# Layer 0's slots turned in 32x32 blocks by VectorE from rows loaded in four pieces, gate and up weights in longer rows, and the two numbers of a row loaded apart in layers 2 and 3

## The chip, the cores and the metric

The kernel runs on one core of one Trainium2 chip. The time is the device time of one execution in microseconds. A core has TensorE (PE, matrix products; its weight loads are listed apart as PEld), VectorE (DVE), ScalarE (ACT), GpSimd (POOL) and SyncE (SP), which here only issues DMAs. Each of them runs its own list of instructions in order, and semaphores hold an instruction back until what it needs is there. Sixteen DMA engines move data between HBM, the on-chip memory of 128 partitions, and back. TensorE contracts over partitions, so it needs activations with channels on partitions ("channel-major"), while rows of a token lie in HBM with a token's channels side by side.

## The reference, cut to what matters

Four layers run on x of 2 x 1024 tokens with 256 channels. Each layer has a conditioning part (a modulation by a vector, attention, or a conditional mixture of experts) and a feed-forward part that is a mixture of experts. Layer 0's feed-forward part is the one that the change reaches most:

```python
topk_ids = jnp.argmax(logits, axis=-1)          # one of E = 32 experts for each of 2048 tokens
xs = x * jax.nn.sigmoid(jnp.max(logits, -1))[:, None]
sorted_x = xs[jnp.argsort(topk_ids)]
g = grouped_mm(sorted_x, routed_gate_w, tokens_per_expert)   # (256 -> 512), called r1
u = grouped_mm(sorted_x, routed_up_w, tokens_per_expert)     # (256 -> 512), called r3
d = grouped_mm(silu(g) * u, routed_down_w, tokens_per_expert)# (512 -> 256), called r2
out = shared_expert(x) + d[argsort(order)]
```

Three more mixtures have the same frame, rows sorted by expert, a small network for each expert, and rows returned to their tokens: layer 2's conditioning (8 experts, two for each token, GELU with 256 hidden channels), layer 2's feed-forward part (8 experts, two for each token, SwiGLU with 1024 hidden channels), and layer 3's conditioning (8 experts, two for each token, GELU with 256 hidden channels).

## The kernel before

**Rows and slots.** Every mixture works on slots of 128 rows. GpSimd scatters token rows into the HBM buffer `xbuf` (`Rows.scatter`, L402). A row has DR = 258 numbers: 256 channels, and two more that say in layers 2 and 3 where the result belongs and whose expert it is. Layer 0 is static: each of its 32 experts owns 96 rows, which makes 24 slots; a token too many goes through a branch (`slots_over`) that is not taken with these inputs. Slots of the other layers are assigned as the routing falls: 35 run in layer 2's conditioning (cph, cpo in the profile), 33 in its feed-forward part, 37 in layer 3's conditioning.

**Loading and turning.** `Slots.fetch` (L1881) loads the 128 x 258 rows of a slot on SyncE's queue (`Rows.load`, L418) into one of four buffers xs. `Slots.rows` (L1889) turns them: two transposes of 128 x 128 on TensorE by `_channel_major` (L500, ps_cm in PSUM), and one VectorE copy out of PSUM (L1895, xsT, three buffers). In layers 2 and 3 two small VectorE operations for each slot then form the row numbers that the result is scattered to: sn (L1899) and sdst (L1902, five buffers), both read from the same buffer xs. `Slots.put` stores a layer 0 result to `ybuf` on ScalarE's queue (L1909), or scatters one of layers 2 and 3 to `tbuf` on GpSimd's.

**Layer 0's order.** `Split.slot` writes TensorE's order by hand: for slot i the gate product fpg (L2081), the up product fpu, then the down product fpo of slot i-1 (L2099), then the turn ps_cm of slot i+2 (L500), then fpt (L2089), four transposes of the product fa of slot i; some preparation of layer 1 is spliced in. VectorE makes fa (L2118), the copy xsT (L1895) and half of faT (L2092); ScalarE makes the SiLU fsg (L2114), the other half of faT and ys (L2103). VectorE also builds layer 1's mask meanwhile (l_ne L901, l_any L903, l_d). The order of VectorE's own instructions is left to a scheduler, which follows what each of them depends on.

**Layer 0's weights.** `ahead` (L553) streams 96 units of 512 KB (gate, up and down of 32 experts) through 22 buffers named ring, XT and HT in the profile, all on SyncE's queue (L559), 21 of them before the first slot. Every unit covers 128 partitions; gate and up lie there as two rows of 2 KB to a partition, down as four of 1 KB.

**Layers 2 and 3.** `Series.slot` is the loop: rows of slot n+2 are fetched, slot n+1 is turned, the weights of slot n are loaded (`_expert_load`, L1865, only for an expert that no set holds), then come the products of slot n. `_gelu_products` (cph L1976, cpo L1983, ys L1985) serves the two conditioning mixtures, `_ffn_products` (L2000 to L2009) and `_mixed_products` layer 2's feed-forward part.

Of the kernel before, what the change touches and what calls it, by code (L numbers as in the profile page):

```python
# [9 lines left out]
F32 = mybir.dt.float32  # L10
I32 = mybir.dt.int32
U32 = mybir.dt.uint32
# [29 lines left out]
class Ring:  # L42


    def __init__(self, t, n):
        self.t, self.n, self.i, self.held = t, n, 0, set()
# [339 lines left out]
class Rows:  # L386
# [30 lines left out]
    def load(self, dst, src):  # L417
        i = self.k.nc.sync.dma_start(dst, src)  # L418
        _after(self.k, i, self.new)
        self.read.append(i.ins.name)  # L420
        return i
# [70 lines left out]
    return ps.rearrange("p c d -> p (c d)")  # L492


def _channel_major(k, psum, rows, ref=None, made=None):


    ps = psum.tile([P, 2, P], F32, name="ps_cm", tag="t", bufs=2)
    for c in range(2):
        i = k.nc.tensor.transpose(ps[:, c, :], rows[:, c * P:(c + 1) * P], k.ident)  # L500
        if ref is not None:
            _behind(k, i, ref)
        if made is not None:
            made.append(i)
    return ps
# [19 lines left out]
def _layer0(k):  # L525
# [14 lines left out]
    def weights(src):  # L540
        ws = [k.ring.take().rearrange("p (c f) -> p c f", f=f) for f in (F, F, D)]
        for w, n in zip(ws, ("L0_r1", "L0_r3", "L0_r2")):
            sent.append(nc.sync.dma_start(w, A[n][src].rearrange("o (c p) f -> p (o c) f", p=P)))
        return ws


# [6 lines left out]
    def ahead(free, ref=None):  # L553

        while todo and 3 * todo[0][0] + todo[0][1] - len(units) < free:
            e, j = todo.pop(0)
            n, f = kinds[j]
            w = ws[e][j] = units[(3 * e + j) % len(units)].rearrange("p (c f) -> p c f", f=f)
            sent.append(nc.sync.dma_start(w, A[n][e].rearrange("(c p) f -> p c f", p=P)))  # L559
            if ref is not None:  # L560
                _behind(k, sent[-1], ref)

    with ExitStack() as ctx:
# [93 lines left out]
        _layer1_loads0(k, k.pre)  # L657
        ahead(-2)
        slots = Slots(k, pool, psum, ref=sent[-1])
        split = Split(k, pool, psum, slots, F, NS)  # L660
        muls = []
        mask = _mask_rows(k, k.pre, pool, psum, muls)
        pre = chain(_layer1_pre(k, k.pre, psum, split.stage), _router_biases(k, psum, split.stage))
        for i in range(NS):
            if i < 18 and i % 2 == 1:
                next(mask)
            lo, cols = i * T, []
            while lo < (i + 1) * T:

                e = lo // C  # L670
                n = 64 if i % 3 == 1 else 32
                cols.append((slice(lo - i * T, lo - i * T + n), ws[e]))
                lo += n
            muls.append(split.slot(i, cols))
            next(pre, None)

            ahead(3 * (i * T // C), slots.load)
        with k.tc.issue_after(split.up.ins):
            k.tc.mark_branch_hint_location('rare', 'LikelyTaken', [mybir.EngineType.PE])
        assert next(pre, pre) is pre and not todo  # L680
# [1192 lines left out]
class Slots:  # L1873

    def __init__(self, k, pool, psum, of=None, base=0, ref=None):
        self.k, self.pool, self.psum, self.of, self.base, self.ref = k, pool, psum, of, base, ref
        self.xs, self.dst = {}, {}

    def fetch(self, i):  # L1881

        if i not in self.xs:
            self.xs[i] = self.pool.tile([P, DR], F32, name="xs", bufs=4)
            self.load = self.k.x.load(self.xs[i], self.k.xbuf[i * P:(i + 1) * P, :])
            if self.ref is not None:
                _behind(self.k, self.load, self.ref)

    def rows(self, i, made=None):  # L1889

        k, nc, pool = self.k, self.k.nc, self.pool
        self.fetch(i)
        xs = self.xs.pop(i)
        xT = pool.tile([P, 2, P], F32, name="xsT", bufs=3)
        turned = nc.vector.tensor_copy(xT, _channel_major(k, self.psum, xs, made=made))  # L1895
        if self.of is not None:

            n = pool.tile([P, 1], F32, name="sn", bufs=3)
            j = nc.vector.tensor_tensor(n, xs[:, D + 1:D + 2], self.of[:, i:i + 1], ALU.not_equal)  # L1899
            _behind(k, j, turned)  # L1900
            self.dst[i] = pool.tile([P, 1], U32, name="sdst", bufs=5)
            j = nc.vector.scalar_tensor_tensor(self.dst[i], xs[:, D:D + 1], -float(self.base), n,  # L1902
                                               ALU.add, ALU.add)
            _behind(k, j, turned)
        return xT

    def put(self, i, y):
        if self.of is None:
            self.k.nc.scalar.dma_start(self.k.ybuf[i * P:(i + 1) * P, :], y)  # L1909
        else:  # L1910

            self.k.t.scatter(y, self.dst.pop(i), bounds_check=2 * N - 1, oob_is_err=False)


class Series:
# [1 line left out]

    def __init__(self, k, slots, ids):  # L1920
        self.k, self.slots, self.ids = k, slots, list(ids)
        self.xT, self.last, self.old, self.soon = {}, None, None, False
        self.fetch(0)
        self.fetch(1)
        self.turn(0)

    def stage(self, insts):

        for i in insts:
            if self.last is not None:  # L1930
                _behind(self.k, i, self.last)
        self.last = insts[-1]

    def fetch(self, n):
        if n < len(self.ids):
# [8 lines left out]
    def slot(self, i, products, weights, soon=False):  # L1944

        n = self.ids.index(i)
        self.fetch(n + 2)
        self.turn(n + 1)
        if self.soon:
            self.close()  # L1950
        self.soon = soon
        p = products(self.xT.pop(i), *weights())
        self.stage(next(p))
        self.close()
        part = next(p)
        while part is not None:
            self.stage(part)
            self.part = part
            part = next(p)
        self.old = i, p  # L1960
# [101 lines left out]
class Split:  # L2062
# [9 lines left out]
    def stage(self, insts):  # L2072

        for i in insts:
            if self.last is not None:
                _behind(self.k, i, self.last)
        self.last = insts[-1]

    def product(self, name, xT, cols, j):
        ps = self.psum.tile([P, self.F], F32, name=name, tag="mm")  # L2080
# [58 lines left out]
def _cond_moe(k, name, wr, bias, W1, W3, W2, nf, hold, R1, R2, gate_mult, final, lead, most, next=None):  # L2139
# [70 lines left out]
        shared(tb, hook, lead_.mid, between=lead_.between)  # L2210
    gate, eid, of, used = lead_.finish()
    k.t.begin()
    by = Slots(k, pool, psum, of, base)

    def slots(lo, hi):
        series = Series(k, by, range(lo, hi))
        for i in range(lo, hi):
            series.slot(i, _gelu_products(k, pool, psum), lambda: _slot_weights(k, eid, i, sets, E))
        series.close()
# [41 lines left out]
def _layer2_ffn(k):  # L2261
# [55 lines left out]
        shared(tb, lead.hook, lead.mid, lead.between)  # L2317
    gate, eid, of, used, mid = lead.finish()
    k.t.begin()
    by = Slots(k, pool, psum, of, base)  # L2320

    def weights(i):
        to = sets[i % 2] if i < MOST - 1 else sets[(i + 1) % 2]
# [3 lines left out]
        return [_expert_load(k, mid, 3 * m + q, sets[j], E) for q, j in enumerate(to) if j is not None]  # L2327

    def slots(ids):
        series = Series(k, by, ids)  # L2330
        for n, i in enumerate(ids):
            if i == NS:
                series.slot(i, _mixed_products(k, pool, psum), lambda: mixed(0, 0, 1, 2), True)
            elif i > NS:
                series.slot(i, _mixed_products(k, pool, psum), lambda: [ahead[0], *mixed(1, None, 0, 1)],
                            True)
            else:
                series.slot(i, _ffn_products(k, pool, psum, 2), lambda: weights(i))
            if i == 8:
                ahead = mixed(1, 2)  # L2340
            if i == MOST - 1:
                with k.tc.issue_after(series.part[len(series.part) // 2].ins):
                    k.tc.mark_branch_hint_location('l2f', 'LikelyTaken', [mybir.EngineType.PE])
        series.close()
# [15 lines left out]
class Last:  # L2360
# [535 lines left out]
```

## Time and profile before

| what | value |
|---|---|
| median of 10 executions | 1414.31 us (1411.46 to 1418.48) |
| the profiled execution | 1415.73 us, its span 1414.0 us |
| mean granted clock of TensorE | 0.988 |
| TensorE busy | 1364.5 us, 96% |
| VectorE, ScalarE, GpSimd busy | 33%, 21%, 19% |
| layer 0's slots, TensorE in 177 to 212 us | 35.00 of 35 us, DMA share 1.05 |
| layer 2's conditioning slots, 441.08 to 512.0 us | TensorE 68.36 of 70.92 us |
| layer 3's conditioning slots, 1176.89 to 1252.81 us | TensorE 72.61 of 75.92 us |

The profiled execution is one execution; its span runs from the first to the last instruction, and the rest of its time lies outside. In the views below a line of the timeline has a start and a length in microseconds, the engine, the line of the kernel, the operation, what it writes and reads, and in brackets how long the engine was idle before it and what ended that. A line of the busy times has the stretch, its length, then each engine's busy time with its number of instructions, the granted clock, the mean busy share of the 16 DMA engines (which can pass 1, as overlapping packets count twice), and the rate. A line of the waits has what waited for what, the total, the number of waits and the longest.

### The profile page before, as it was taken

The page shows a single profiled execution, that of the slowest core. Times are in us where ns is not written, and L with a number is a line of the kernel's source. Part 1 is how long each engine was busy: PE and PEld are TensorE (multiplying, and loading weights), DVE is VectorE, ACT ScalarE, POOL GpSimd, SP SyncE. Part 2 cuts the span into 40 slices and gives each one's busy share as a digit, 9 for nine tenths or more (in the row PEclk, how much of TensorE's full clock was granted, in tenths as well). Part 3 has the DMA queues.
Part 4 walks back from the last instruction along what each step waited for, and adds up shares of the span by engine and source line. Part 5 has one row for each costly group of instructions (what it writes and reads, how often), then busy time and mean ns, then how long its engine had stood idle before and what let it go on. Part 6 is the DMA issues. An engine that isn't in the chain of part 4 may idle for free. (4 is left out here: it accounts for less than half of the span.)

```text
span 1414.0 us, 23096 instructions
## 1 busy us (share of the span) xinstructions
PE 1364.5 (96%) x8431; PEld 955.8 (68%) x8431; DVE 461.5 (33%) x1519; ACT 302.1 (21%) x636; POOL 273.1 (19%) x308
## 2 busy tenths in 40 slices
PE   9999999999999999999999999999999979998897
PEld 4544444655657876555599999999956548875685
DVE  3523322325313443511211111111115503458432
ACT  3212221234112112111111111111112212127121
POOL 0410001300432430142000001000100262430441
PEclk9999999999999999999999999999999989999899
DMA  9879992933313861081375365366338346748570
GB/s 309 309 236 348 357 367 76 305 84 135 113 52 88 254 201 54 29 314 61 101 286 206 111 209 205 118 235 226 119 117 299 115 137 213 239 148 281 196 236 16
DMA packets 185424, 265.26 MB, mean 188 GB/s; under 512 B 16759, under 2 KB 134655, under 8 KB 185296
## 3 DMA queue, kind: packets, MB, share of 16 engines
q1 hardware_dynamic: 163984, 221.65, 47.6%
q0 software_dynamic: 13744, 36.63, 7.3%
q10 hardware_dynamic: 7568, 5.34, 1.2%
q8 instruction: 71, 1.16, 0.3%
q14 instruction: 57, 0.47, 0.1%
HBM read 283.67 MB, written 46.82 MB: 234 GB/s over the span
## 5 line engine op out<-in xcount | busy, mean ns | idle before, releaser
L402 POOL DMA_INDIRECT tbuf<-ys,sdst x105 | 103.3, 984 | 466.8 <-ACT ys L2012 300.9
L1675 PE MATMUL spo<-ring,sa 128*128 128x256 f32 x704 | 167.7, 384 | 9.6 <-DVE sa L1703 9.5
L1675 PEld LDWEIGHTS spo<-ring,sa 128*128 128x128 f32 x704 | 134.2, 193 | 56.3 <-issue 28.3
L1703 DVE TENSOR_TENSOR sa<-ssg,spu 128x512 f32<-128x512 f32 x88 | 60.3, 686 | 248.6 <-PE spu L1690 203.3
L2005 DVE TENSOR_TENSOR fa<-fsg,fpu 128x512 f32<-128x512 f32 x62 | 42.6, 688 | 278.3 <-PE fpu L2000 278.3
L2000 PE MATMUL fpg<-xsT,ring 128*128 128x128 f32 x992 | 121.1, 275 | 1.0 <-DMA ring<-in_L_w 1.0
L2000 PE MATMUL fpu<-xsT,ring 128*128 128x128 f32 x992 | 121.0, 275 | 0.6 <-DMA ring<-in_L_w 0.6
L2000 PEld LDWEIGHTS fpg<-xsT,ring 128*128 128x128 f32 x992 | 117.9, 192 | 3.5 <-issue 2.0
L2000 PEld LDWEIGHTS fpu<-xsT,ring 128*128 128x128 f32 x992 | 115.7, 192 | 0.7 <-issue 0.7
L1699 ACT ACTIVATE ssg<-spg 128x512 f32<-128x512 f32 x88 | 52.5, 597 | 282.0 <-PE spg L1690 220.0
L2009 PE MATMUL fpo<-ring,fa 128*128 128x256 f32 x496 | 112.4, 380 | 0.0
L2009 PEld LDWEIGHTS fpo<-ring,fa 128*128 128x128 f32 x496 | 91.9, 190 | 12.1 <-issue 0.8
L1690 PE MATMUL spg<-HT,ring 128*128 128x512 f32 x192 | 92.8, 598 | 4.1 <-issue 2.2
L1690 PE MATMUL spu<-HT,ring 128*128 128x512 f32 x192 | 91.2, 598 | 0.0
L1976 PE MATMUL cph<-xsT,ring 128*128 128x128 f32 x576 | 77.5, 277 | 5.9 <-DVE sn L1899 2.6
L1690 PE MATMUL spg<-XT,ring 128*128 128x512 f32 x160 | 75.6, 594 | 1.3 <-DVE ys L1985 1.2
L1976 PEld LDWEIGHTS cph<-xsT,ring 128*128 128x128 f32 x576 | 70.1, 192 | 9.3 <-DVE sn L1899 4.1
L1690 PE MATMUL spu<-XT,ring 128*128 128x512 f32 x160 | 75.4, 592 | 0.0
L1983 PE MATMUL cpo<-ring,ch 128*128 128x256 f32 x288 | 73.8, 380 | 0.0
L2004 ACT ACTIVATE fsg<-fpg 128x512 f32<-128x512 f32 x62 | 37.0, 597 | 143.8 <-PE fpg L2000 142.5
L1690 PEld LDWEIGHTS spu<-HT,ring 128*128 128x128 f32 x192 | 36.7, 193 | 45.1 <-issue 44.9
L1895 DVE COPY xsT<-ps_cm 128x256 f32<-128x256 f32 x129 | 53.8, 418 | 30.5 <-PE ps_cm L500 30.5
(677 smaller groups left out, 1761.8 us busy)
## 6 DMA issues: line engine op xcount, KB each, us to landing
ring<-in_L_w SPq DMA_DIRECT2D x105, 1024.0 KB
ring<-in_L_r SPq DMA_DIRECT2D x72, 512.0 KB
ring<-in_L_r SPq DMA_DIRECT2D x144, 256.0 KB
xs<-xbuf SPq DMA_DIRECT2D x129, 129.0 KB
ring<-in_L_W SPq DMA_DIRECT2D x32, 512.0 KB
yt<-tbuf SPq DMA_DIRECT2D x48, 256.0 KB
XT<-in_L_r SPq DMA_DIRECT2D x16, 512.0 KB
HT<-in_L_r SPq DMA_DIRECT2D x8, 512.0 KB
```

The lines of the kernel that those rows point to most:

```text
L402: i = k.nc.gpsimd.indirect_dma_start(out=self.ap, out_offset=bass.IndirectOffsetOnAxis(ap=idx, axis=0), in_=rows, in_offset=None, **end)
L1675: mm = nc.tensor.matmul(po[g // 2][:, g % 2, :], a[:, g * P:(g + 1) * P], W2[:, f, :], start=f == 0 and g % 2 == 0, stop=f == nf - 1, skip ...
L1690: mm = nc.tensor.matmul(ps, W[:, c, f * P:(f + 1) * P], X[:, c, cols], start=c == 0, stop=c == 1)
L1699: k.silu = nc.scalar.activation(sg, pg, AF.Silu)
L1703: mul = nc.vector.tensor_mul(a, sg, pu)
L1895: turned = nc.vector.tensor_copy(xT, _channel_major(k, self.psum, xs, made=made))
L1976: made = [nc.tensor.matmul(ph[:, f, :], R1[:, c, f * P:(f + 1) * P], xT[:, c, :], start=c == 0, stop=c == 1) for f in range(2) for c in ra ...
L1983: made = [nc.tensor.matmul(po, h[:, f, :], R2[:, f, :], start=f == 0, stop=f == 1) for f in range(2)]
L2000: made = [nc.tensor.matmul(ps[:, j, :], W[:, c, (f0 + j) * P:(f0 + j + 1) * P], xT[:, c, :], start=c == 0, stop=c == 1) for ps, W in ((pg, ...
L2004: nc.scalar.activation(sg, pg, AF.Silu)
L2005: nc.vector.tensor_mul(a[:, f0:f0 + 4, :], sg, pu)
L2009: made = [nc.tensor.matmul(po, a[:, f, :], W2[:, f, :], start=f == 0, stop=f == 4 * nh - 1) for f in range(4 * nh)]
```

## The change

The change has four edits.

1. *Layer 0's turn.* Slots 2 to 23 are loaded by four DMAs instead of one. DMA q brings channels 64q to 64q+63 of all 128 rows to the 32 partitions 32q to 32q+31, four pieces of 256 B to a partition (`xq`). One VectorE transpose, which turns every 32x32 block in place, then writes xsT directly. The TensorE transposes and the PSUM copy of these slots are gone. Partition p now holds channels 2p and 2p+1, and so slots 0 and 1, which stay on TensorE, read every second channel (`pairs`).
2. *Weights.* Gate and up of layer 0 are laid down to match: one row of 4 KB to a partition. Down is as before.
3. *Numbers.* In layers 2 and 3 (`blocks=False`, so TensorE still turns) a row load brings 256 channels. The two numbers of all rows of a stage come in one DMA (`numbers`, called once after the turn of the stage's second slot), 128 partitions by 39 or 41 slots by 8 B, in a buffer of the xs pool; two VectorE operations form all row numbers of the stage at once, and each scatter uses a column of them.
4. *Fetching.* `Series.slot` asks for the rows of slot n+3 behind the weights of slot n.

```diff
 def _channel_major(..., pairs=False):
-        i = k.nc.tensor.transpose(ps[:, c, :], rows[:, c * P:(c + 1) * P], k.ident)
+        i = k.nc.tensor.transpose(ps[:, c, :], rows[:, c::2] if pairs else rows[:, c * P:(c + 1) * P], k.ident)
...
-            sent.append(nc.sync.dma_start(w, A[n][e].rearrange("(c p) f -> p c f", p=P)))
+            form = "(c p) f -> p c f" if n == "L0_r2" else "(p c) f -> p c f"
+            sent.append(nc.sync.dma_start(w, A[n][e].rearrange(form, p=P)))
...
         slots = Slots(k, pool, psum, ref=sent[-1])
+        slots.plan(range(NS), (0, 1), 1)
...
     def fetch(self, i):
-        if i not in self.xs:
-            self.xs[i] = self.pool.tile([P, DR], F32, name="xs", bufs=4)
-            self.load = self.k.x.load(self.xs[i], self.k.xbuf[i * P:(i + 1) * P, :])
...
+        if group is None:
+            self.xs[i] = self.pool.tile([P, D], F32, name="xs", bufs=4)
+            self.load(self.xs[i], k.xbuf[i * P:(i + 1) * P, 0:D])
+            return
+        lo, n = group
+        if self.of is None:
+            t = self.pool.tile([P, n, 4, 64], F32, name="xq", tag="xs", bufs=4)
...
+        for q in range(4):
+            self.load(t[32 * q:32 * q + 32, 0:n].rearrange("p g b k -> p (g b) k"),
+                      k.xbuf[lo * P:(lo + n) * P, 64 * q:64 * q + 64].rearrange("(b s) k -> s b k", s=32))
...
     def rows(self, i, made):
-        turned = nc.vector.tensor_copy(xT, _channel_major(k, self.psum, xs, made=made))
-        if self.of is not None:
-            n = pool.tile([P, 1], F32, name="sn", bufs=3)
-            j = nc.vector.tensor_tensor(n, xs[:, D + 1:D + 2], self.of[:, i:i + 1], ALU.not_equal)
-            _behind(k, j, turned)
-            self.dst[i] = pool.tile([P, 1], U32, name="sdst", bufs=5)
-            j = nc.vector.scalar_tensor_tensor(self.dst[i], xs[:, D:D + 1], -float(self.base), n,
-                                               ALU.add, ALU.add)
+        if self.group[i] is None:
+            self.turned = nc.vector.tensor_copy(xT, _channel_major(k, self.psum, xs, made=made, pairs=self.blocks))
+        else:
+            self.turned = nc.vector.transpose(xT.rearrange("p c (b s) -> p c b s", b=4),
+                                              xs.rearrange("p b (r c) -> p c b r", c=2))
...
+    def numbers(self):
+        k, nc, n = self.k, self.k.nc, self.of.shape[1]
+        m = self.pool.tile([P, n, 2], F32, name="xm", tag="xs", bufs=4)
+        k.x.load(m, k.xbuf[0:n * P, D:].rearrange("(i p) d -> p i d", p=P))
+        i = nc.vector.tensor_tensor(m[:, :, 1], m[:, :, 1], self.of, ALU.not_equal)
+        _behind(k, i, self.turned)
+        self.dst = k.rp.tile([P, n], U32, name="sdst", tag="sdst")
+        nc.vector.scalar_tensor_tensor(self.dst, m[:, :, 0], -float(self.base), m[:, :, 1], ALU.add, ALU.add)
...
     def slot(self, i, products, weights, soon=False):
         n = self.ids.index(i)
         self.fetch(n + 2)
         self.turn(n + 1)
+        if self.slots.of is not None and self.slots.dst is None:
+            self.slots.numbers()
...
         p = products(self.xT.pop(i), *weights())
+        self.fetch(n + 3)
...
-    by = Slots(k, pool, psum, of, base)
+    by = Slots(k, pool, psum, of, base, blocks=False)
```

More of the change, by code (lines that the diff above doesn't have):

```diff
@@ L492, in _token_major, with _channel_major @@
     return ps.rearrange("p c d -> p (c d)")
-def _channel_major(k, psum, rows, ref=None, made=None):
+def _channel_major(k, psum, rows, ref=None, made=None, pairs=False):
     ps = psum.tile([P, 2, P], F32, name="ps_cm", tag="t", bufs=2)
     for c in range(2):
-        i = k.nc.tensor.transpose(ps[:, c, :], rows[:, c * P:(c + 1) * P], k.ident)
+        i = k.nc.tensor.transpose(ps[:, c, :], rows[:, c::2] if pairs else rows[:, c * P:(c + 1) * P], k.ident)
         if ref is not None:
@@ L542, in weights @@
         for w, n in zip(ws, ("L0_r1", "L0_r3", "L0_r2")):
-            sent.append(nc.sync.dma_start(w, A[n][src].rearrange("o (c p) f -> p (o c) f", p=P)))
+            form = "o (c p) f -> p (o c) f" if n == "L0_r2" else "o (p c) f -> p (o c) f"
+            sent.append(nc.sync.dma_start(w, A[n][src].rearrange(form, p=P)))
         return ws
@@ L675, in _layer0 @@
             next(pre, None)
-            ahead(3 * (i * T // C), slots.load)
+            ahead(3 * (i * T // C), slots.loaded)
         with k.tc.issue_after(split.up.ins):
@@ L1873, with __init__, plan, load @@
 class Slots:
-    def __init__(self, k, pool, psum, of=None, base=0, ref=None):
+    def __init__(self, k, pool, psum, of=None, base=0, ref=None, blocks=True):
         self.k, self.pool, self.psum, self.of, self.base, self.ref = k, pool, psum, of, base, ref
-        self.xs, self.dst = {}, {}
-    def fetch(self, i):
-        if i not in self.xs:
-            self.xs[i] = self.pool.tile([P, DR], F32, name="xs", bufs=4)
-            self.load = self.k.x.load(self.xs[i], self.k.xbuf[i * P:(i + 1) * P, :])
-            if self.ref is not None:
-                _behind(self.k, self.load, self.ref)
-    def rows(self, i, made=None):
+        self.xs, self.group, self.dst, self.blocks = {}, {}, None, blocks
+    def plan(self, ids, rows, most):
+        ids = list(ids)
+        while ids:
+            n = 1
+            if ids[0] in rows or not self.blocks:
+                self.group[ids[0]] = None
+            else:
+                while n < most and ids[n:n + 1] == [ids[0] + n]:
+                    n += 1
+                for j in range(n):
+                    self.group[ids[j]] = ids[0], n
+            ids = ids[n:]
+    def load(self, t, src):
+        self.loaded = self.k.x.load(t, src)
+        if self.ref is not None:
+            _behind(self.k, self.loaded, self.ref)
+    def fetch(self, i):
+        if i in self.xs:
+            return
+        k, group = self.k, self.group[i]
+        if group is None:
+            self.xs[i] = self.pool.tile([P, D], F32, name="xs", bufs=4)
+            self.load(self.xs[i], k.xbuf[i * P:(i + 1) * P, 0:D])
+            return
+        lo, n = group
+        if self.of is None:
+            t = self.pool.tile([P, n, 4, 64], F32, name="xq", tag="xs", bufs=4)
+        else:
+            t = self.pool.tile([P, 2, 4, 64], F32, name="xq", tag="yt", bufs=5)
+        for q in range(4):
+            self.load(t[32 * q:32 * q + 32, 0:n].rearrange("p g b k -> p (g b) k"),
+                      k.xbuf[lo * P:(lo + n) * P, 64 * q:64 * q + 64].rearrange("(b s) k -> s b k", s=32))
+        for j in range(n):
+            self.xs[lo + j] = t[:, j]
+    def rows(self, i, made):
         k, nc, pool = self.k, self.k.nc, self.pool
@@ L1894, in rows @@
         xT = pool.tile([P, 2, P], F32, name="xsT", bufs=3)
-        turned = nc.vector.tensor_copy(xT, _channel_major(k, self.psum, xs, made=made))
-        if self.of is not None:
-            n = pool.tile([P, 1], F32, name="sn", bufs=3)
-            j = nc.vector.tensor_tensor(n, xs[:, D + 1:D + 2], self.of[:, i:i + 1], ALU.not_equal)
-            _behind(k, j, turned)
-            self.dst[i] = pool.tile([P, 1], U32, name="sdst", bufs=5)
-            j = nc.vector.scalar_tensor_tensor(self.dst[i], xs[:, D:D + 1], -float(self.base), n,
-                                               ALU.add, ALU.add)
-            _behind(k, j, turned)
-        return xT
+        if self.group[i] is None:
+            self.turned = nc.vector.tensor_copy(xT, _channel_major(k, self.psum, xs, made=made, pairs=self.blocks))
+        else:
+            self.turned = nc.vector.transpose(xT.rearrange("p c (b s) -> p c b s", b=4),
+                                              xs.rearrange("p b (r c) -> p c b r", c=2))
+        return xT
+    def numbers(self):
[6 more added lines that the diff above has]
+        nc.vector.scalar_tensor_tensor(self.dst, m[:, :, 0], -float(self.base), m[:, :, 1], ALU.add, ALU.add)
     def put(self, i, y):
@@ L1910, in put, with __init__ @@
         else:
-            self.k.t.scatter(y, self.dst.pop(i), bounds_check=2 * N - 1, oob_is_err=False)
+            self.k.t.scatter(y, self.dst[:, i:i + 1], bounds_check=2 * N - 1, oob_is_err=False)
 class Series:
-    def __init__(self, k, slots, ids):
+    def __init__(self, k, slots, ids, rows=0):
         self.k, self.slots, self.ids = k, slots, list(ids)
         self.xT, self.last, self.old, self.soon = {}, None, None, False
+        slots.plan(ids, self.ids[:rows], 1 if slots.of is None else 2)
         self.fetch(0)
@@ L1931, in stage @@
                 _behind(self.k, i, self.last)
-        self.last = insts[-1]
+        self.last = (insts or [self.last])[-1]
     def fetch(self, n):
@@ L2076, in stage @@
                 _behind(self.k, i, self.last)
-        self.last = insts[-1]
+        self.last = (insts or [self.last])[-1]
     def product(self, name, xT, cols, j):
@@ L2212, in _cond_moe @@
     k.t.begin()
-    by = Slots(k, pool, psum, of, base)
+    by = Slots(k, pool, psum, of, base, blocks=False)
     def slots(lo, hi):
-        series = Series(k, by, range(lo, hi))
+        series = Series(k, by, range(lo, hi), 0 if lo else 2)
         for i in range(lo, hi):
@@ L2319, in _layer2_ffn @@
     k.t.begin()
-    by = Slots(k, pool, psum, of, base)
+    by = Slots(k, pool, psum, of, base, blocks=False)
     def weights(i):
@@ L2329, in slots @@
     def slots(ids):
-        series = Series(k, by, ids)
+        series = Series(k, by, ids, 1 if ids[0] == NS else 0)
         for n, i in enumerate(ids):
```

## The prediction

> **What bounds the kernel now.** I read the page first, then the busy time of each engine by stretch, then the timeline of the last slots of layer 0 and of the first slots of layer 3's mixture, and last the waits of SyncE's queue. From the page:
>
> ```profile
> PE 1364.5 (96%) x8431; PEld 955.8 (68%) x8431; DVE 461.5 (33%) x1519; ACT 302.1 (21%) x636; POOL 273.1 (19%) x308
> PE   9999999999999999999999999999999979998897
> DMA  9879992933313861081375365366338346748570
> q10 hardware_dynamic: 7568, 5.34, 1.2%
> ```
>
> TensorE is the bound nearly everywhere. Layer 0's slots (slices 2 to 6) have both TensorE and the DMA engines full, so a microsecond off TensorE there counts only while weights keep up. Busy time by stretch (columns: stretch, length, PE, PEld, DVE, ACT, POOL, clock, DMA share, GB/s):
>
> ```profile
> 7.00:10.00 3.00, 2.15 (x11) 1.57 (x12) 2.65 (x10) 0.21 (x1) 0.00 (x0) 1.00 1.06 403
> 177.00:212.00 35.00, 35.00 (x342) 14.93 (x336) 10.12 (x24) 7.30 (x16) 0.00 (x0) 1.00 1.05 368
> 250.00:266.00 16.00, 16.00 (x57) 9.78 (x56) 6.72 (x14) 3.08 (x7) 8.37 (x9) 1.00 1.14 298
> 441.08:512.00 70.92, 68.36 (x475) 61.87 (x474) 35.42 (x137) 14.91 (x36) 31.49 (x32) 1.00 0.67 208
> 1176.89:1252.81 75.92, 72.61 (x504) 65.58 (x503) 37.18 (x145) 15.67 (x38) 33.47 (x34) 1.00 0.71 226
> ```
>
> Layer 0 has no PE gap (177 to 212); the slots of layers 2 and 3 (last two lines) have gaps of 2.6 and 3.3 us. The turns that move, in the timeline (start, length, engine, line):
>
> ```profile
> 200.75 1.94 PE L2081 MATMUL fpg<-ring,xsT 128*64 128x512 f32 x8
> 206.20 0.44 PE L500 MATMUL ps_cm<-ident,xs 128*128 128x128 f32 x2
> 206.67 0.42 DVE L1895 COPY xsT<-ps_cm 128x256 f32<-128x256 f32 x1 [1.48 <-PE ps_cm L500]
> 207.00 1.92 PE L2081 MATMUL fpg<-ring,xsT 128*32 128x512 f32 x16
> ...
> 219.36 0.64 PE L2081 MATMUL fpg<-XT,xsT 128*64 128x512 f32 x1
> 224.81 0.66 PE L2089 MATMUL fpt<-ident,fa 128*128 128x128 f32 x4
> 225.39 0.62 PE L2081 MATMUL fpg<-HT,xsT 128*32 128x512 f32 x1
> 225.50 0.42 DVE L2092 COPY faT<-fpt 128x256 f32<-128x256 f32 x1 [1.70 <-PE fpt L2089]
> ```
>
> The copy at 206.67 is for a slot that starts over 6 us later: today the turned rows are a slot ahead. Also needed are the spacing of two mask operations on VectorE, the start of layer 3's slots, and SyncE's waits (total, times, longest):
>
> ```profile
> 161.69 0.42 DVE L901 TENSOR_TENSOR l_ne<-l_mm,l_m 128x256 int32<-128x256 int32 x1
> 162.15 0.42 DVE L903 TENSOR_TENSOR l_any<-l_any,l_ne 128x256 int32<-128x256 int32 x1
> ```
> ```profile
> 1173.64 5.42 SPq L418 DMA_DIRECT2D xs<-xbuf  x6
> 1179.26 0.42 DVE L1895 COPY xsT<-ps_cm 128x256 f32<-128x256 f32 x1 [0.80 <-PE ps_cm L500]
> 1181.04 1.06 PE L1976 MATMUL cph<-xsT,ring 128*128 128x128 f32 x8
> ```
> ```profile
> SPq L418 <- DVE sdst L1902: 70.3, 43, 23.9
> ```
>
> **Part 1, TensorE's turns in layer 0.** 22 of 24 slots lose their ps_cm pair. Slots 19 and 22 have the same column split: 19, with a pair, runs 200.75 to 207.00 = 6.25 us; 22, the first without one (no slot 24 exists), 219.36 to 225.39 = 6.03. Saved 0.22 a slot, 22 x 0.22 = **-4.8 us**. Bounds: slot 21 (6.11) against 22 gives 0.08, -1.8; the pair's own 0.44 gives -9.7. I take 0.22, the like-for-like pair.
>
> The Trainium skill, "VectorE: DVE Perf Modes", section "The three transpose paths", gives 390 ns for a 128x128 bf16 transpose on TensorE and 311 ns on VectorE, the latter in 32x32 blocks only. By it TensorE would save 22 x 2 x 0.39 = 17 us (an estimate), but it prices a transpose alone; the trace shows the pair overlapped with its neighbours.
>
> **Part 2, the turn on VectorE.** The new instruction reads what the DMA laid down, so the schedule no longer ties it to a place on TensorE. In the built order it slips: up to slot 10 it stands one or more products ahead of need, but from slot 11 slot n's turn comes after the product fa(n-1), just before slot n's fpg, which waits for it. Behind fa(n-1) alone it is covered by fpo(n-2) (1.93 us). For n = 14, 20, 23 it stands behind faT(n-1) too: faT starts 0.69 after fpt (224.81, 225.50), the turn 0.34 later (spacing of 206.67's kind of copy), ends 0.42 on, and PE starts 0.06 after: fpt + 1.51, where fpg comes now at + 0.58. That is 0.93 each, 2.8. For n = 11 and 17 two mask operations (0.46 and 0.34 more) stand between: 1.7 each, 3.4. n = 19 stands behind layer 1's l_d chain, which waits for PE: about 0.7. Sum **+6.9 us**. Its duration is not in the trace; nearest are the 128x256 f32 copy and int32 operation, both 0.42, which I take. Bounds: 0.33 (the shortest 128x256 spacing), and 0.84 (two of them), which adds 6 x 0.42 = 2.5. If the scheduler's places do not bite, 0. Bounds 0 to +9.4. The 22 PSUM copies go, and cost nothing: DVE is 10.12 of 35 busy.
>
> **Part 3, DMA in layer 0.** A slot's rows become 512 pieces of 256 B in four DMAs on 32 partitions. At 403 GB/s a 2 KB row takes 2048 x 16 / 403 = 81 ns per engine; at 298 GB/s, in the stretch of 512 B rows, 27.5. The line through both is 10 ns a descriptor plus 0.035 ns/B. So (512 - 128) x 10 / 16 = +0.24 us a slot. ACT's queue gives a dearer end: 1.2% x 16 x 1414 / 7568 = 36 ns each, which would make it 0.86. Against it, gate and up in 4 KB rows save 256 descriptors an expert, 341 a slot: -0.21. Net about 0 to +0.65 us of 6.25 a slot, up to 14 in all. The last weight is issued at 207.43 and needed at 225.39, about 14 us after landing, and SyncE waits for PE before weights (35.8 us in 17 waits): **0**. SyncE issues three more DMAs a slot, about 0.4 each, beside four weights of 0.45 to 1.1: full, but not over 6 us. At the start 14 row issues stand before the HT weights instead of 5, at 0.58 (2.91 / 5): those weights are 5 us later, of 14 us slack; slot 2's pieces land about 77.70 + 6 x 0.58 + 2.15 = 83.3 (2.15 from issue to PE today), and VectorE needs them before fa0 at 84.58. If all this cover went, +1 to +6.
>
> The Trainium skill, "DMA: Bandwidth & Descriptors", section "Rules for kernel authors", says that transfers to separate parts of the partitions serialize and advises one over 128; its "Specifications" ask for at least 512 B for line rate. Both speak against this edit. No row here has 256 B pieces at full load, so the descriptor line above decides the sum, and the page's advice would only raise the risk of starving.
>
> **Part 4, the numbers in layers 2 and 3.** Each stage now loads the two numbers of all slots with one DMA of 4992 or 5248 pieces of 8 B, 313 or more an engine, and VectorE's one pair on them stands before the turn of slot 2. So cph(2) and all of VectorE wait for its landing. Per piece: 10 ns (line), 15.5 (ACT's queue less its 1 KB rows: (271 - 233) us / 2448), 36 (its mean): 3.3, 4.9, 11.3 us, and 2.15 to land. In layer 3's slots it is issued about 1175.0 and needed by about 1180.25 (VectorE's turn, copy and hand-over take 0.8 before 1181.04): late by 0.2, 1.8 or 8.2. I take **+1.8**. Layer 2's cond slots have 10.7 us of cover (0; 2.7 at 36 ns), its ffn 24 (0).
>
> Gone are 105 pairs of small VectorE operations and their waits. A slot's sdst waited for an old scatter to finish, and so held its xs buffer and SyncE's queue (70.3 us over 43 waits). What TensorE lost by this is unclear: an undisturbed slot of the cph stages takes 1.98 us from cph to cph (1179.06 to 1181.04), and against that the two stages lose 3.6 and 4.7 = 8.3 us. The gaps lie where every slot brings new weights and the DMA share is 1.0 or more (1.00 to 1.07 between 1184 and 1202 and 1216 and 1228), so they are lack of bandwidth; a queue freed sooner only starts such a burst sooner, by what sdst held it (SyncE's longest such wait there is 1.8 us). Bounds 0 to -8.3; I take **-1.5**, less than one such hold per stage. The extra fetch(n+3) keeps the order of rows and weights on SyncE as it was: 0. The 105 turns there stay on PE.
>
> **Sum**: -4.8 + 6.9 + 0 + 1.8 - 1.5 = +2.4. The profiled execution took 1415.73 (span 1414.0, 1.73 outside it); it would take 1418.1. It lies 1.42 above the median 1414.31, so I forecast 1416.7.
>
> **Rivals.** (a) Faster: the freed queue. If sdst's release recovers over 6.7 of the 8.3 us, the sum falls below -2.8; all of it gives -4.4, 1409.9. For it: 70.3 us of waits; against: PE's own gaps on sn are 2.6 us on the page. (b) The 8 B pieces cost 36 ns: 8.2 + 2.7 in place of 1.8, 1425.8. For it: ACT's mean; against: that mean holds 1 KB rows. (c) Weights starve in layer 0: +1 to +6, 3.5 in the middle, 1420.2. For it: DMA share 1.05; against: 14 us of slack. (d) The late turns don't stall, because hardware reaches them sooner than the order suggests or they are short: 1414.3 - 4.8 + 1.8 - 1.5 = 1409.8; with the stalls under 1.7 us it ends below -2.8. For it: VectorE is idle for two thirds of layer 0; against: the order of the built program. (e) The change does not do what it says, TensorE's time per slot not falling since weights set the pace: 4.8 more, 1421.5; for it, the full DMA row of 177 to 212, against it, SyncE's waits for PE. It is counted with (c).
>
> **How the numbers follow.** About 0.2% either way (2.8 us) can be told from no change. Forecast 0.45 (0.22 slower, 0.23 same, as its sum lies beside the bound); (a) 0.13 (0.11 faster, 0.02 same); (b) 0.16, slower; (c) with (e) 0.12 (0.10 slower, 0.02 same); (d) 0.14 (0.11 faster, 0.03 same). Together faster 0.22, same 0.30, slower 0.48. The range 1409.0 to 1424.0 leaves out most of (b) and the ends of (a) and (d) in which bounds add up. The forecast's own range is 1413.5 to 1420.5.
>
> **What would show it.** After: PE gaps before fpg of slots 11, 14, 17, 19, 20, 23, released by VectorE's transpose; slots with an early turn near 6.03; no fpg released by DMA (else c); layer 3's cph(2) released by sdst or xm's DMA; SyncE's wait for sdst near 0. The forecast is wrong if the transpose takes over 0.84 us, if pieces cost other than 10 to 15 ns, or if the gaps of the later slots close.

## The result

The changed kernel takes 1439.14 us (median of 8 runs, 1434.78 to 1442.04); the kernel before, beside it, 1414.61 (28 runs). The ratio is 1.0171, 95% interval 1.0157 to 1.0184: slower by some 24 us. The forecast was 1416.7, with a range up to 1424.0. The profiled execution took 1439.78 us, its span 1438.1.

The page of the changed kernel, in the lines that answer to those shown before:

```profile
PE 1368.0 (95%) x8387; PEld 953.7 (66%) x8387; DVE 434.0 (30%) x1315; ACT 302.1 (21%) x636; POOL 273.3 (19%) x308
PE   9999787999999999999999999999999978998897
DMA  9858888793222663082284556256448346848570
```

TensorE now idles in slices 5 to 7, which are the second half of layer 0's slots; before, every one of them was 9. The DMA row fell from 9 to 8 in slices 4 to 6, and in slice 7 it is 8 where it was 2: the same weights arrive over a longer time. So the DMA engines did not become the bound: they are less busy than before while TensorE waits. The busy times by stretch say the same (columns as before). First two stretches of the kernel before, of which the prediction shows the third (1.05, 368 GB/s):

```profile
106.00:141.00 35.00, 35.00 (x362) 16.25 (x362) 11.98 (x34) 9.94 (x20) 0.00 (x0) 1.00 1.02 348
141.00:177.00 36.00, 36.00 (x352) 15.39 (x345) 11.51 (x24) 7.74 (x18) 0.00 (x0) 1.00 1.04 357
```

Then the changed kernel:

```profile
106.00:141.00 35.00, 35.00 (x362) 15.56 (x362) 10.53 (x31) 10.08 (x19) 0.00 (x0) 1.00 0.83 279
141.00:177.00 36.00, 28.39 (x264) 11.47 (x252) 8.66 (x18) 6.11 (x14) 0.00 (x0) 0.98 0.78 255
177.00:212.00 35.00, 30.29 (x235) 11.71 (x239) 7.57 (x16) 5.37 (x12) 0.00 (x0) 0.87 0.88 296
212.00:252.00 40.00, 32.36 (x290) 13.34 (x282) 8.98 (x22) 6.71 (x15) 0.00 (x0) 1.00 0.84 276
```

From the starts of products in the two timelines, the 24.1 us between the spans come from these places:

| stretch | before, us | after, us | difference |
|---|---|---|---|
| span's start to slot 0's fpg | 80.78 | 81.22 | +0.4 |
| fpg of slot 0 to fpg of slot 23 | 144.61 | 171.40 | +26.8 |
| from there to layer 2's first cph | 216.68 | 212.68 | -4.0 |
| layer 2's cond slots, first to last cph | 69.93 | 68.16 | -1.8 |
| between the two cph stages | 665.88 | 666.34 | +0.5 |
| layer 3's cond slots | 74.93 | 76.98 | +2.1 |
| the rest | 161.19 | 161.32 | +0.1 |

Not all of the 26.8 us in the slots is waiting. From slot 0's to slot 23's fpg TensorE is idle for 21.5 us (0.5 before). Beside that the profile shows half the clock granted in two stretches, where before it was 1.00 through all these slots:

```profile
175.87:182.70 6.83, 5.61 (x28) 1.57 (x32) 0.45 (x1) 0.60 (x1) 0.00 (x0) 0.50 1.03 311
203.18:206.59 3.41, 3.09 (x16) 0.92 (x20) 0.17 (x1) 0.00 (x0) 0.00 (x0) 0.50 1.02 393
```

Slot 14, in which TensorE never idles, has 5.6 us of this and takes 8.79 us, against 6.04 in the fourth experiment below. Half of the 10.2 us, some 5 us (an estimate), is thus lost to the clock and not to a wait. In the profiles in which rows and weights come in time (the kernel before and the first, third, fifth, sixth, seventh and ninth experiments) no such stretch lies in the slots; which wait brings it on was not tried.

The waits of SyncE's queue, then those of TensorE, between 80 and 256 us of the changed kernel (total, times, longest):

```profile
SPq L418 <- DMA ybuf<-ys: 44.2, 8, 8.1
SPq L561 <- DMA ybuf<-ys: 17.0, 6, 7.4
...
PE fpg L2124 <- DVE xsT L1932: 15.3, 5, 4.6
PE fpg L2124 <- DMA ring<-in_L_r: 2.4, 2, 2.2
PE fpg L2124 <- issue: 1.6, 1, 1.6
```

SyncE, which loads rows (L418) and weights (L561), spends 61 us waiting for ybuf, the stores of results that ScalarE's queue makes, although no row and no weight needs a result. One such wait in full, from the timeline of SyncE's queue and of the engines that follow from it:

```profile
160.69 5.45 SPq L561 DMA_DIRECT2D ring<-in_L_r  x6
166.25 7.92 SPq L418 DMA_DIRECT2D xq<-xbuf  x4
174.21 1.47 SPq L561 DMA_DIRECT2D ring<-in_L_r  x3
...
176.50 0.45 DVE L1932 STREAM_TRANSPOSE xsT<-xq 128x256 f32<-128x256 f32 x1 [2.48 <-DMA xq<-xbuf]
177.09 1.93 PE L2124 MATMUL fpg<-ring,xsT 128*32 128x512 f32 x8 [3.54 <-DVE xsT L1932]
```

SyncE's longest wait between 160 and 176 us:

```profile
SPq L418 <- DMA ybuf<-ys: 5.6, 1, 5.6
```

Four row DMAs of 0.4 us each take 7.92 us, because the third stands 5.6 us for a store. In the built program every DMA that SyncE or ScalarE issues has one of eight semaphores that tell of its landing, taken in rotation by both engines together; the trace shows the same eight on both queues. A DMA waits until the one that last used its semaphore has landed, which is the one some eight places back. The third row DMA here, issued at 173.38, takes the semaphore of the store that ScalarE issued at 166.51. Its pieces land late, VectorE turns late, and TensorE stands 3.54 us. The weights behind it on the queue are held too.

With one row DMA a slot some six DMAs belong to a slot (one of rows, four of weights, one store), so that SyncE could be more than a slot ahead of the store it waits for; with four there are nine, and eight places are less than a slot. Before, the same wait was in the profile (stretch 80 to 232, SyncE), but SyncE had the lead to bear it:

```profile
SPq L559 <- DMA ybuf<-ys: 14.6, 8, 4.4
```

This is the theory "shared semaphores". Its rivals are "late turns" (the prediction's own part 2), "pieces" (256 B pieces fill the DMA engines) and "weights" (the longer weight rows).

### The profile page after: what moved, and what is told of

It reads as the page before. It is cut to its first block, busy times and chain, and to the rows that moved or that the text cites. A ratio compares the mean times of both kernels' runs of the same rounds, so it can differ in the third digit from the quotient of the medians.

```text
span 1438.1 us, 22941 instructions
## 1 busy us (share of the span) xinstructions
PE 1368.0 (95%) x8387; PEld 953.7 (66%) x8387; DVE 434.0 (30%) x1315; ACT 302.1 (21%) x636; POOL 273.3 (19%) x308
## 5 line engine op out<-in xcount | busy, mean ns | idle before, releaser
L2028 DVE COPY ys<-cpo 128x256 f32<-128x256 f32 x72 | 30.6, 425 | 93.5 <-PE cpo L2026 78.2
```

The costliest lines, as they stand in the source:

```text
L2028: nc.vector.tensor_copy(y, po)
```

## The experiments

**Stores from GpSimd.** In the built program GpSimd's DMAs take no part in this rotation (they have eight other semaphores), so this takes the stores out of it.

```diff
     def put(self, i, y):
         if self.of is None:
-            self.k.nc.scalar.dma_start(self.k.ybuf[i * P:(i + 1) * P, :], y)
+            self.k.nc.gpsimd.dma_start(self.k.ybuf[i * P:(i + 1) * P, :], y)
```

> The changed kernel, with layer 0's result stores (ybuf) issued from GpSimd instead of ScalarE. Theory 'shared semaphores': in the built program every DMA of SyncE and ScalarE waits for the DMA that stands eight places earlier in one common rotation; with four row DMAs a slot, SyncE reaches a result store that has not been written yet, stops there (44.2 + 17.0 us of its waits name ybuf) and issues weights late. Taking the stores out of the rotation should give back most of the 24.5 us: 1417 to 1427. Rival 'late turns': PE waits because VectorE's turn stands behind other work; no change, 1437 to 1441. Rival 'pieces': the 256 B pieces fill the DMA engines; no change, 1437 to 1441.

Measured: 1418.69 us beside 1417.29, ratio 1.0012 (0.9994 to 1.0030). Of 24 us, about 23 are gone. "Pieces" and "weights" fall as main causes: both are still in. What is left shows the late turns by themselves. TensorE's waits for them between 80 and 256 us, which lie before slots 11, 14, 17, 20 and 23, and then the end of slot 18:

```profile
PE fpg L2124 <- DVE xsT L1932: 6.4, 5, 1.8
```
```profile
200.17 0.69 DVE L2161 TENSOR_TENSOR fa<-fsg,fpu 128x512 f32<-128x512 f32 x1 [2.46 <-PE fpu L2124]
...
201.22 0.15 DVE L909 TENSOR_SCALAR l_d<-l_d 128x1 f32<-128x1 f32 x1
...
201.43 0.38 PE L911 MATMUL l_pd<-l_d,ones 128*128 128x1 f32 x2
...
201.85 0.16 DVE L913 COPY l_differf<-l_pd 128x1 f32<-128x1 f32 x1 [0.47 <-PE l_pd L911]
...
202.29 0.14 DVE L687 CAST l_rare<-l_raref 1x1 int32<-1x1 f32 x1
202.47 0.45 DVE L1932 STREAM_TRANSPOSE xsT<-xq 128x256 f32<-128x256 f32 x1
202.74 0.66 PE L2132 MATMUL fpt<-ident,fa 128*128 128x128 f32 x4
203.33 1.51 PE L2124 MATMUL fpg<-ring,xsT 128*64 128x512 f32 x6
```

In slot 18 the turn stands behind fa and the l_d chain, as the prediction read it from the built order. But slot 19's fpg does not wait for this turn: it comes 0.59 us behind fpt, as in a slot without a stall. The slot's 1.0 us is lost earlier, where TensorE's own step of the chain (l_pd, L911) stands in the middle of fpo and needs l_d: fpt starts 6.35 us after the slot's fpg, and 5.30 in the fourth experiment, in which no l_d stands in this slot.

**The number of DMAs alone, without pieces and without VectorE's turn.** The kernel before, its rows in four DMAs of 32 whole rows.

```diff
-            self.load = self.k.x.load(self.xs[i], self.k.xbuf[i * P:(i + 1) * P, :])
...
+            for q in range(4 if self.of is None else 1):
+                r = slice(32 * q, 32 * q + 32) if self.of is None else slice(0, P)
+                self.load = self.k.x.load(self.xs[i][r, :], self.k.xbuf[i * P + r.start:i * P + r.stop, :])
```

> The kernel before, with each slot's rows in layer 0 loaded by four DMAs of 32 whole rows instead of one of 128 (same 128 rows of 1032 B, turns on TensorE, everything else as before). Shared semaphores: the number of DMAs alone costs most of the loss, 1426 to 1438. Late turns and pieces: nothing of theirs is in it, 1413 to 1416.

Measured: 1440.27 us beside 1417.29 (4 runs), ratio 1.0173 (1.0134 to 1.0213), just above the expected range. The number of DMAs makes as large a loss by itself, with old pieces, old weight rows and old turns. (3.5 of TensorE's 18.2 us below lie before slot 0's first product; the clock is below 1 here too.) The waits between 80 and 256 us of TensorE and SyncE, and two stretches:

```profile
PE ps_cm L500 <- DMA xs<-xbuf: 18.2, 7, 4.4
...
SPq L418 <- DMA ybuf<-ys: 31.7, 6, 7.0
```
```profile
177.00:212.00 35.00, 29.39 (x252) 12.52 (x256) 10.92 (x27) 5.75 (x13) 0.00 (x0) 0.95 0.93 306
212.00:251.00 39.00, 33.28 (x300) 13.38 (x296) 6.83 (x13) 6.36 (x14) 0.00 (x0) 0.91 0.71 235
```

**All turns on TensorE, the other edits kept.**

```diff
-        slots.plan(range(NS), (0, 1), 1)
+        slots.plan(range(NS), range(NS), 1)
```

> The changed kernel, with all 24 slots of layer 0 loaded by one DMA and turned on TensorE (every second channel), all its other edits kept: gate and up in 4 KB rows, numbers apart, fetch(n+3). All three theories of the rows: layer 0 takes its old time, and what is left is -1.8 us of layer 2's cond slots and +2.0 of layer 3's, 1412 to 1417. Rival 'weights': the longer weight rows are the cause, 1435 to 1440.

Measured: 1416.90 us beside 1417.29, ratio 0.9997 (0.9980 to 1.0014). The long weight rows, the numbers apart and fetch(n+3) together move nothing that can be told. "Weights" falls.

**Rows from GpSimd.** The four row DMAs leave SyncE, the stores stay on ScalarE.

```diff
     def load(self, dst, src, eng=None):
-        i = self.k.nc.sync.dma_start(dst, src)
+        i = (eng or self.k.nc.sync).dma_start(dst, src)
...
-                      k.xbuf[lo * P:(lo + n) * P, 64 * q:64 * q + 64].rearrange("(b s) k -> s b k", s=32))
+                      k.xbuf[lo * P:(lo + n) * P, 64 * q:64 * q + 64].rearrange("(b s) k -> s b k", s=32), k.nc.gpsimd)
```

> The changed kernel, with the four row DMAs of a slot issued from GpSimd, outside the rotation that SyncE and ScalarE share; pieces, VectorE turns and all else kept. Shared semaphores: SyncE has only weights left and runs ahead as before; the turns' 4.8 us come off and late turns may cost up to 6.9: 1410 to 1418. Late turns alone: 1435 or more, as the turns stay where VectorE has them. Pieces: 1435 or more.

Measured: 1413.09 us beside 1417.29, ratio 0.9977 (0.9956 to 0.9998). All 256 B pieces and VectorE turns are in, and the kernel is as fast as before or a little faster. Its stretches in layer 0:

```profile
110.00:145.00 35.00, 35.00 (x384) 15.87 (x380) 12.33 (x36) 9.86 (x19) 10.88 (x20) 1.00 1.05 360
145.00:177.00 32.00, 32.00 (x300) 12.89 (x296) 9.78 (x22) 7.47 (x17) 12.28 (x23) 1.00 1.05 363
```

TensorE is full and the DMA engines move 360 to 363 GB/s, what they moved before (348 to 368 GB/s). The pieces cost nothing that can be seen. In this build the scheduler also put every turn early enough: TensorE waits for none. The lengths of single slots, from fpg to fpg in microseconds, show the parts side by side:

| slot | before | after | stores from GpSimd | rows from GpSimd |
|---|---|---|---|---|
| 0 | 5.35 | 5.35 | 5.36 | 7.05 |
| 10 | 6.26 | 7.86 | 7.86 | 6.04 |
| 11 | 6.25 | 6.35 | 6.03 | 6.04 |
| 12 | 6.10 | 9.10 | 5.89 | 5.88 |
| 13 | 6.26 | 10.50 | 7.06 | 6.03 |
| 14 | 6.25 | 8.79 | 6.04 | 6.04 |
| 16 | 6.37 | 10.78 | 7.86 | 6.47 |
| 18 | 6.10 | 7.15 | 6.93 | 5.89 |
| 19 | 6.25 | 10.19 | 7.06 | 6.03 |
| 20 | 6.25 | 7.74 | 6.04 | 6.04 |
| 22 | 6.03 | 8.68 | 7.07 | 6.04 |
| slots 0 to 22 | 144.61 | 171.40 | 147.71 | 142.05 |

The last column is 0.21 to 0.23 under the first in slots 10 to 14: TensorE's turn, as costed. The third column is long before slots 11, 14, 17, 19, 20 and 23 and nowhere else. Slot 0 of the last column, 7.05 us, has as much TensorE idle time as in the changed kernel (0.91 us), but 3.41 us of it ran at half the granted clock.

**Stores from GpSimd and every turn a slot early.**

```diff
         mul = nc.vector.tensor_mul(a, sg, pu)
+        if self.slots.turned is not None:
+            _behind(self.k, mul, self.slots.turned)
```

> The kernel of the first experiment (changed kernel, stores from GpSimd), with one ordering added: the product fa of slot i stands behind the turn of slot i+1 on VectorE, so that no turn comes later than a slot ahead of its need. Late turns: six slots in the first experiment are longer by 1.0 to 1.8 us, 7.3 in sum; they go, 1418.7 - 7.3 = 1411.4, 1409 to 1414. Rival 'weights': TensorE in those slots would have waited for weights anyway; 1417 to 1420, with waits for the ring in place of waits for xsT.

Measured: 1414.77 us beside 1417.83, ratio 0.9978 (0.9958 to 0.9999). Slots 10, 13, 16 and 19 fall to 6.03 or 6.04. Slots 18 and 22 stay long (7.17 and 7.13), because fa now stands behind a late turn: in slot 22 its rows have only just landed (VectorE is idle 4.94 us for xq before it), in slot 18 the turn stands behind the l_d chain, for whose step on TensorE VectorE is idle 2.86 us. The slots 0 to 22 take 142.31 us, 5.4 less than without the ordering. Against the kernel before, the ratio went from 1.0012 to 0.9978, about 4.8 us, of the 7.3 expected, and the median is just above the expected range.

**Rows from GpSimd, early turns, slot 2 on TensorE.** The ordering above in the fourth experiment's kernel, and slot 2's rows in one DMA.

```diff
-        slots.plan(range(NS), (0, 1), 1)
+        slots.plan(range(NS), (0, 1, 2), 1)
...
         mul = nc.vector.tensor_mul(a, sg, pu)
+        if self.slots.turned is not None:
+            _behind(self.k, mul, self.slots.turned)
```

> The kernel of the fourth experiment (rows from GpSimd), with the same ordering, and slot 2 loaded by one DMA and turned on TensorE as slots 0 and 1, since its first product waited for the first GpSimd loads (slot 0 there took 7.05 us, and 5.35 before the change). Late turns: the fourth experiment shows none, so the ordering gains nothing; the start gains 1.7 less 0.2 for the turn: 1410 to 1413 beside 1413.1 there. Rival: GpSimd's loads still come late at the start; 1412 to 1415.

Measured: 1415.59 us beside 1417.83, ratio 0.9987 (0.9968 to 1.0005). This is above the expected 1410 to 1413. Slot 0 is back at 5.35, with no half clock in it, and the slots 0 to 22 take 140.35, 4.3 less than before the change, but the whole kernel is not better than with the fourth experiment's edit (0.9977), within what these intervals tell. Neither interval reaches a gain of more than 0.5%.

**Numbers apart and fetch(n+3) alone.** The changed kernel with layer 0's slots and weights as before.

```diff
-        slots = Slots(k, pool, psum, ref=sent[-1])
+        slots = Slots(k, pool, psum, ref=sent[-1], blocks=False)
...
-            form = "(c p) f -> p c f" if n == "L0_r2" else "(p c) f -> p c f"
+            form = "(c p) f -> p c f"
```

> The kernel before with the last two edits alone: numbers apart in layers 2 and 3, and fetch(n+3); layer 0's rows in one DMA, turned on TensorE, weights in rows of 2 KB. By the prediction's terms +1.8 (the wait for the 8 B pieces in layer 3) and -1.5 (the release of sdst): no change within what can be told, 1414 to 1419 beside a before of 1414 to 1418; layer 2's cond slots near 68.1 us instead of 69.9, layer 3's near 76 instead of 74.3. Rival: one of the two is all of it; 2 us up or down.

Measured: 1417.81 us beside 1415.90, ratio 1.0018 (1.0002 to 1.0034). In its profile layer 2's cond slots take 69.47 us (68.1 expected) and layer 3's 76.36. This is at most a small loss, and it is not the 24 us.

**The second experiment with stores from GpSimd.** On the kernel before:

```diff
+            for q in range(4 if self.of is None else 1):
+                r = slice(32 * q, 32 * q + 32) if self.of is None else slice(0, P)
...
-            self.k.nc.scalar.dma_start(self.k.ybuf[i * P:(i + 1) * P, :], y)
+            self.k.nc.gpsimd.dma_start(self.k.ybuf[i * P:(i + 1) * P, :], y)
```

> The kernel of the second experiment (before, with rows in four DMAs of 32 whole rows, 1440.3 us), with the result stores issued from GpSimd. Shared semaphores: the stores were what SyncE stood at, and the 23 us go: 1414 to 1420. Rival 'eight in flight': small DMAs take places from weights in the rotation whatever the stores do; 1430 to 1440.

Measured: 1422.17 us beside 1415.90, ratio 1.0034 (1.0019 to 1.0048). Of the 24 us of four whole-row loads, some 20 go with the stores. A rest of some 5 us stays, and the time is above the expected 1414 to 1420. In its profiled execution, which was a long one (span 1427.1), TensorE still waits 5.2 us in 3 times for rows, 3.1 of them before slot 0's first product and 2.1 in slot 21, and half the clock is granted for 6.5 us of slots 0 and 22; whether that is the rotation's eight places without any store, or SyncE's own issue time, was not told apart.

**Stores from GpSimd on the kernel before.**

```diff
-            self.k.nc.scalar.dma_start(self.k.ybuf[i * P:(i + 1) * P, :], y)
+            self.k.nc.gpsimd.dma_start(self.k.ybuf[i * P:(i + 1) * P, :], y)
```

> The kernel before, with only the result stores issued from GpSimd. Shared semaphores: SyncE's waits for ybuf (14.6 us in 8 waits before weights) go, but weights were early already: no change, 1413 to 1418. Rival: the store's move itself is worth something (a gain that the first experiment then owed to it): 1405 to 1411.

Measured: 1418.82 us beside 1415.90, ratio 1.0013 (0.9995 to 1.0031). SyncE's waits for ybuf are gone from the profile, and the move gains nothing by itself, so what the first experiment gave back it owed to the held queue.

## Why the prediction was wrong

The prediction was wrong in part 3, at one step: "SyncE issues three more DMAs a slot, about 0.4 each, beside four weights of 0.45 to 1.1: full, but not over 6 us", and with it the **0** for DMA. It counted how long SyncE is busy issuing, and the bytes and descriptors, and found both within the 14 us of slack. It did not ask what each new issue waits for. The term measured about +23: 1440.27 against 1417.29 us with the number of loads alone changed. Part of it, some 5 us in the changed kernel, is the halved clock beside the waits, for which the prediction had no term. The row for it was there: SyncE's waits for ybuf, 14.6 us in 8 waits, which no data explains. Such a row means that a queue is tied to another engine's progress, and it should have been followed to its semaphore.

Rival (c) named the outcome, weights and rows late in layer 0, but by a lack of bandwidth and at +1 to +6. The DMA share went down, from 1.05 to 0.78 to 0.88, which speaks against bandwidth, and the experiment with GpSimd's rows moves the same pieces at 360 GB/s.

The Trainium skill, "DMA: Bandwidth & Descriptors", section "Rules for kernel authors", advised one transfer over 128 partitions rather than several over parts. The runs agree with its advice (1.0173 for four in place of one), though not with its reason: what the four cost here was places in a rotation of semaphores, not engine time. The same page, in "Anatomy of one DMA — SWDGE (gpsimd) path", says that a wait on a semaphore is made by the issuing engine ahead of the dispatch; this case shows what follows, a wait of 5.6 us in which nothing behind it on SyncE's queue could start.

The other steps held in size, two of them with a qualification:

- *TensorE's turns*, -4.8 at 0.22 a slot. Slots with early turns are 6.03, 6.04 and 5.88 us where they were 6.25, 6.26 and 6.10.
- *Late turns*, +6.9. With the stores out of the way, just the six slots named are longer. Against the fifth experiment's 6.03 to 6.04 (fourth's 5.89 and 6.04 for slots 18 and 22) they lose 1.8, 1.0, 1.8, 1.0, 1.0 and 1.0, 7.8 in sum; the l_d chain was put at 0.7 and took 1.0. That sixth figure is right partly by luck: TensorE waits for the turn before five slots (6.4 us), and in slot 18 it loses the 1.0 us at its own l_pd. The transpose took 0.44 to 0.45 us, taken as 0.42. Rival (d) falls.
- *Numbers*, +1.8 and -1.5. In layer 3 the third cph comes 4.07 us after the first instead of 3.16, so 0.9 in this profile; in the other six kernels with numbers apart it is 0.3 to 2.0 (3.45 to 5.14 us against 3.16), mostly under the 1.8. The chain in the changed kernel:

```profile
1198.01 0.43 SPq L418 DMA_DIRECT2D xm<-xbuf  x1
...
1202.88 0.20 DVE L1941 TENSOR_TENSOR xm<-xm,l3c_of 128x39 f32<-128x39 f32 x1 [2.72 <-DMA xm<-xbuf]
...
1203.40 0.42 DVE L1930 COPY xsT<-ps_cm 128x256 f32<-128x256 f32 x1
1203.87 0.97 PEld L2019 LDWEIGHTS cph<-xsT,ring 128*128 128x128 f32 x8 [0.16 <-DVE xsT L1930]
```

  The DMA took 4.9 us from issue to use, not 13.5 as rival (b) would have it. Layer 2's cond slots gained (69.4 to 72.1 us in the four profiles with numbers slot by slot, 67.5 to 69.7 in the seven with numbers apart), and layer 3's lost (73.4 to 75.0 against 74.3 to 77.9), some 2 us each way by the means (70.3 and 68.3, 74.2 and 76.1), so rival (a) falls as well. That the two cancel was forecast; what layer 3's slots lost beyond the late third cph was not traced.

Without part 3 the sum was +2.4 us; the first experiment's kernel, which has everything but the held queue, measured 1.0012, which is +1.7 us (-0.8 to +4.2).

After the slots 4.0 us came back that no step foresaw. 2.2 of them are a gap in TensorE that the profile of before puts down to issue, ahead of the first shared product after the slots. The changed kernel does not have it; experiment three, with all turns on TensorE, has 2.1. Its cause was not tried. The other 1.7 are the clock: in the profile of before half of it was granted for 3.41 us from 237.23, just behind that gap, and in this part of the changed kernel it was 1.00. Experiment nine has the gap without the half clock, and takes 214.93 us there, 2.2 more than the changed kernel.

## What to carry to other kernels

Count a split DMA not only in bytes, descriptors and issue time, but in what each issue must wait for: where DMAs of two engines share a few semaphores in rotation, each additional one shortens the lead of a prefetching queue, and a slow store on another engine's queue can then stop it. A wait in the profile between two things that share no data (loads for a store) is the sign, even while it costs nothing. Read the granted clock of the stretch beside the waits: here they cost more than their own length. When a queue loses its lead, move either the many small loads or the stores to a queue that is outside the rotation, and then look at what the scheduler made of the order, since an instruction that lost its old tie may come just too late.

## What the runs showed that was not expected

- A store of 128 KB from ScalarE, issued at 166.51 us behind six weight loads of 512 KB (issued 160.69 to 166.14), released SyncE's next row DMA only at 173.38, nearly 7 us later. Ahead of the slots, in the kernel before, a row load was used 2.15 us after its issue.
- GpSimd issued four row DMAs in 2.18 us and kept layer 0 fed, with TensorE busy 35.00 of 35 us, while VectorE worked 12.33.
- With all turns on TensorE, reading every second channel as weights made a slot 0.07 us longer (6.32 against 6.25 us in slots 10 and 11, third and seventh experiment). The weight rows differ between them too, but slot 22, beside which no turn runs, takes 6.04 and 6.03 us.
- The granted clock fell to half inside layer 0's slots in each of the three profiles whose rows came late in them (the changed kernel, the second and the eighth experiment), and one slot without any wait lost 2.75 us by it.
